# Selective scans on one core: two x buffers, one evacuation per projection, y summed in column quarters, and zero products counted at two passes

## The chip, the cores and the metric

One core of a Trainium2 chip runs the whole program. The metric is device time in microseconds of one execution: 15255.39 us as the median of three runs (15252.08 to 15267.42). The core has a TensorE (PE) for matrix products, a VectorE (DVE), a ScalarE (ACT), a GpSimd (POOL) and a SyncE (SP, which issues most DMAs). Each engine takes its instructions in the order in which the program stands for it, so one instruction that waits holds up all that stand behind it on that engine.

## The reference, cut to what matters

The model has four layers on `x` of shape 4 x 64 x 64 x 96. Layers 0 and 1 hold nearly all of the time: each runs four selective scans (in four orders of the 4096 tokens) over 192 channels with 16 states per channel, for 4 images. Layers 2 and 3 and the feed-forward parts come behind the scans and are untouched by the change. The core of a scan, cut from the reference:

```python
xs    = x_flat[:, :, idx[k]]                       # tokens in the order of direction k
dts, Bs, Cs = split(einsum('bkdl,kcd->bkcl', xs, x_proj_weight))
delta = softplus(einsum('bkrl,kdr->bkdl', dts, dt_projs_weight) + bias)
h     = h * exp(delta * A) + (delta * u) * B       # for each token, 192 x 16 states
y     = einsum('bkdn,bkn->bkd', h, C)              # sum over the 16 states
```

In layer 0 (the "ordered" one) the directions are two diagonal snakes and two radial orders, so tokens are gathered and scattered; in layer 1 they are rows and columns, forwards and backwards.

## The kernel before, in words

**Batches, directions, segments, groups.** `Stream.run` makes 8 batches (layer 0 for images 0 to 3, then layer 1 for images 0 to 3). A batch has 4 directions of 4 segments; a segment is 1024 tokens (`SEG`). A segment's 192 x 16 = 3072 state rows are 24 groups of 128 partitions (32 channels by 4 states): 6 channel blocks `cb` by 4 state blocks `sg`. So there are 8 x 16 x 24 = 3072 groups.

**One group** is worked on by all engines in turn. ACT makes the decay `da` (L1072). DVE multiplies the spread input `u` by B into `t` (L1076, `enter`) and runs the recurrence into `h` (L1083, `recur`). ACT keeps the last state (L1094). POOL multiplies `h` by C into `hc` (L1098, `leave`). PE sums `hc` over states into the PSUM tile `y` (L1107, `collect`): two products of 128 x 512, each to one column tile of 32 of the PE array. `y` holds two channel blocks (a pair); after the second, ACT copies it to `yc` (L1136), PE turns it (L1148), ACT copies the rows into `spare` (L1152) and, once a segment, the rows are stored (a plain DMA from SP, or, for the first two directions of layer 0, eight indirect scatters from POOL, L1162). `u` is one PSUM tile with one buffer: PE's `spread` (L1065, two products of 512 columns) for a channel block can start only when DVE has done the last `t` of the block before, and DVE's next `t` waits for it.

**Preparing the next segment** goes on beside this (`prepare`). PE transposes the fetched tokens (L897), ACT copies them into `xs` (L908, or L913 one copy per diagonal run), PE projects (L934: four times two products into the single PSUM tile `m`), ACT evacuates each projection with several reads of `m` (absolute value into `sp_z` L947, positive part into `dt` L949, B and C rows L951 or L953), ACT computes a softplus from these (L991 to L1006), PE adds its four terms (L1014), ACT copies the sum (L1017), SP stores it to DRAM, POOL forms `dtu = dt * x` (L1023). SP then loads `dt` spread over partitions (`dts`) and B and C (`bc`). In the kernel before there is one `xs`, so the first transpose for a segment waits for both `dtu` of the one before.

**Who sets the order.** `Flow.run` writes all orders down when the program is built: it plays a list of operations with a supposed duration (`occ`), a latency, a due time, and a flag `hard` for those of the 24 groups, and each time puts the operation that can start soonest. It is a plan made beforehand; the chip only follows the order. Where PE would be idle for a time `gap` in the plan, `keep_busy` puts products by zero in (L1125: 96 x 32 by 256 columns), which add nothing to `y` and are there to keep PE at work. In the kernel before, their number is `(gap - 0.15) * 0.7 / 0.215`, and there are none while no sum of `y` is open (from the last `collect` of a pair to the first of the next).

**Between batches** (`side_by_side`) another planner (`Plan`) merges the finished batch and makes the front part of a batch to come; its buffers are `z_rows`, `xc`, `y_rows`, `yt`, `dx` and `halo`.

Of the kernel before, what the change touches and what calls it, by code (L numbers as in the profile page):

```python
# [113 lines left out]
class Op:  # L114


    def __init__(self, engine, occ, emit, deps=(), lat=0.15, due=None, hard=False, bank=0, after=0.0):
        self.engine, self.occ, self.emit, self.lat = engine, occ, emit, lat
        self.deps = [d for d in deps if d is not None]
        self.due, self.hard, self.bank, self.after = due, hard, bank, after  # L120
        self.users, self.left, self.seen = [], 0, 0.0


class Flow:
# [11 lines left out]
    def run(self):  # L136
# [22 lines left out]
        while left:  # L159
            best = None  # L160
            for engine, ops in ready.items():
# [7 lines left out]
                if strict and first:  # L169
                    limit = first[-1].due + drift - (3.2 if engine == "PE" else 0.5)  # L170
# [20 lines left out]
            if engine == "PE":  # L191
                self.fill(start - free[engine])
# [4 lines left out]
            free[engine] = start + op.occ  # L197
            done = start + op.occ
# [4 lines left out]
            for user in op.users:  # L203
                user.seen = max(user.seen, done if user.engine == engine else done + op.lat)
                user.left -= 1
                if not user.left:
                    ready[user.engine].append(user)
# [97 lines left out]
class Layer:  # L305


    def __init__(self, s, a, pre, x_in):
# [24 lines left out]
        self.bias_bc = None  # L333
        if self.ordered:
            self.bias_bc = k.t(w, [128, ND], pre + "dir_bc")
            nc.sync.dma_start(self.bias_bc[C:], a[pre + "dirBC"])
        conv_w = k.load(s.seg, a[pre + "conv_w"], "conv_w")
# [39 lines left out]
class Stream:  # L377
# [4 lines left out]
    def __init__(self, k, ctx, a, x, x1, y1):  # L382
# [20 lines left out]
        self.bc = k.t(w, [128, 2, NSG, SEG], "bc")  # L403
        self.zeros = k.t(w, [C, GC], "zeros")
        nc.gpsimd.memset(self.zeros, 0.0)

# [5 lines left out]
    def front(self, bt, plan, rings, first=None):  # L412
# [22 lines left out]
        def edges(s, st):  # L435

            halo = yield from take(self.tmp, [C, 2, HW], "halo", 2)
# [29 lines left out]
        def project(s, st):  # L467
# [31 lines left out]
            def outer(j):  # L499
# [6 lines left out]
                z = yield from take(self.tmp, [C, 2, CH], "z_rows", 2)  # L506
# [19 lines left out]
        def convolve(s, st):  # L526
            yield lambda: st.pad is not None
            xc = []
            for _ in range(C // GC):
                xc.append((yield from take(self.tmp, [128, CH], "xc", 3)))  # L530
# [26 lines left out]
            rows = yield from take(self.tmp, [128, 2, 4, DI], "y_rows", 1)  # L557
# [27 lines left out]
    def merge(self, bt, plan, rings):  # L585
# [29 lines left out]
        def times_d(n):  # L615

            x = yield from take(tmp, [128, T, DI], "dx", 1)
# [73 lines left out]
        def finish(n, acc, mv):  # L691
# [20 lines left out]
            yt = yield from take(tmp, [C, 2, CH], "yt", 1)  # L712
# [35 lines left out]
    def side_by_side(self, ahead, behind=None, flush=None, seg=None):  # L748
# [3 lines left out]
        plan, rings = Plan(), Rings(k)  # L752
        self.ended, self.idle = False, None
# [117 lines left out]
    def prepare(self, seg, base=0.0, before=None):  # L871
# [7 lines left out]
        def op(name, engine, occ, emit, deps=(), at=0.0, **kw):  # L879
            x = Op(engine, occ, emit, deps, due=base + at, **kw)  # L880
# [22 lines left out]
        def keep_x(j, parts):  # L903
            if (j, parts[0]) == (0, 0):
                seg.xs = k.t(self.seg, [C, 2, SEG], "xs")
# [9 lines left out]
        for j in range(0, SEG // 128, 2):  # L915
            here = [f for n, f in enumerate(seg.fetched) if len(seg.fetched) < 4 or seg.turned or n // 2 == j // 2]
            here.append(o.get(("X", j - 2)))
            if j == 0:
                here += [b.get(("u", h)) for h in range(2)]
# [18 lines left out]
        def split(half, j, what):  # L938
            if (half, j, what) == (0, 0, 0):
# [6 lines left out]
            if what == 0:  # L946
                nc.scalar.activation(v.z[:, half, cols], ps[:C], AF.Abs, bias=bias)  # L947
            elif what == 1:
                nc.scalar.activation(v.dt[:, half, cols], ps[:C], AF.Relu, bias=bias)  # L949
            elif lay.bias_bc is None:  # L950
                nc.scalar.copy(v.bc[:, cols], ps[C:])  # L951
            else:
                nc.scalar.activation(v.bc[:, cols], ps[C:], AF.Identity, bias=lay.bias_bc[C:, kd : kd + 1])  # L953

        last, chain = o["xs", SEG // 128 - 2], None
        for half in range(2):
            for j in range(2):
                at = 20.0 + 3.5 * (2 * half + j)
                free = []
                if (half, j) == (0, 0):  # L960
                    free = [b.get(n) for n in (("u", 0), ("u", 1), ("out", 0), ("out", 1), "bc_out", ("sum", 1, 1))]
# [13 lines left out]
                p = op(("z", half, j), "ACT", 0.6, partial(split, half, j, 0), [p], at=at + 2.0)  # L975
                if half == 0:
                    p = op(("z", half, j), "ACT", 0.63, partial(split, half, j, 2), [p], at=at + 3.0)
                op(("z", half, j), "ACT", 0.65, partial(split, half, j, 1), [p], at=at + 4.0, bank=-1)
# [7 lines left out]
        def low(half, what):  # L986
            if (half, what) == (0, 0):
                seg.dtu = k.t(self.seg, [C, 2, SEG], "dtu", bufs=2)
            z, r = v.z, seg.dtu
            if what == 0:  # L990
                nc.scalar.activation(z[:, half], z[:, half], AF.Exp, scale=-1.0)  # L991
            elif what == 1:
# [5 lines left out]
        for half in range(2):  # L998
            p = op(("low", half, 0), "ACT", 1.08, partial(low, half, 0), [o["z", half, 1], p], at=32.0 + 5.0 * half)
            p = op(("low", half, 1), "ACT", 1.08, partial(low, half, 1), [p], at=33.5 + 5.0 * half)  # L1000
            p = op(("low", half, 2), "ACT", 1.08, partial(low, half, 2), [p], at=35.0 + 5.0 * half)
# [6 lines left out]
        op("log", "ACT", 4.6, log, [o["low", 0, 2], o["low", 1, 2], b.get(("sum", 1, 1))], at=42.0)  # L1008
# [91 lines left out]
    def collect(self, gr):  # L1100

        nc, seg, cb = self.nc, gr.seg, gr.cb
        if gr.sg == 0 and cb % 2 == 0:
            seg.y = self.k.t(self.ps_y, [128, CH], "y")
        for part in range(2):
            at = (part * 2 + cb % 2) * GC
            nc.tensor.matmul(  # L1107
                seg.y[at : at + GC, :],
                self.gather_y,
                gr.hc[:, part * CH : (part + 1) * CH],  # L1110
# [4 lines left out]
        self.open = gr if gr.sg < NSG - 1 else None  # L1115

    def keep_busy(self, gap):


        gr = self.open  # L1120
        if gr is None:
            return
        at = gr.cb % 2 * GC
        for _ in range(int((gap - 0.15) * 0.7 / 0.215)):
            self.nc.tensor.matmul(  # L1125
                gr.seg.y[at : at + GC, :256],
                self.zeros,
                gr.seg.bt.lay.diag.rearrange("p h t c -> p (h t c)")[:, :256],
                start=False,
                stop=False,  # L1130
                tile_position=(0, at),
# [6 lines left out]
    def turn(self, seg, pair):  # L1138

        k, nc = self.k, self.nc  # L1140
        if pair == 0:
            seg.rows = self.spare()[:, : SEG // 128 * DI].rearrange("p (f t d) -> p f t d", f=2, d=DI)
        ps = seg.ps = k.t(self.ps, [128, CH // 128, 128], "m")
        fours = seg.bt.lay.ordered or seg.kd % 2 == 0
        for j in range(CH // 128):

            v = seg.ycs[pair][:, j::4] if fours else seg.ycs[pair][:, j * 128 : (j + 1) * 128]
            nc.tensor.transpose(ps[:, j, :], v, k.ident)  # L1148

    def keep_rows(self, seg, pair):  # L1150
        ps = seg.ps.rearrange("p j (f d) -> p f j d", f=2)
        self.nc.scalar.copy(seg.rows[:, :, :, pair * 64 : (pair + 1) * 64], ps)  # L1152

    def store(self, seg):

        nc, ops = self.nc, []
        rows = lambda: seg.rows.rearrange("p f t d -> p (f t) d")
# [11 lines left out]
        def whole():  # L1169
            at = self.start(seg)  # L1170
            dst = to[at : at + SEG, :].rearrange("(f p t) d -> p f (t d)", f=2, t=4)
            nc.sync.dma_start(dst, seg.rows.rearrange("p f t d -> p f (t d)"))
# [4 lines left out]
        if seg.bt.lay.ordered and seg.kd < 2:  # L1177
            return [Op("POOL", 1.25, partial(scatter, j), lat=4.0) for j in range(SEG // 128)]
# [5 lines left out]
    def batch(self, segs):  # L1184
# [15 lines left out]
        for n, seg in enumerate(segs):  # L1200
            base, o, nxt = n * length, seg.o, seg.next
            prev = segs[n - 1] if n else None
            if nxt:
# [3 lines left out]
                nxt.o["low", 0, 0].deps += [prev.o["spread", NCB - 1]] if prev else []  # L1207
# [7 lines left out]
            for i in range(NG):  # L1215
# [44 lines left out]
                for g2 in (groups[n, i - 1], gr):  # L1260
# [24 lines left out]
                    )  # L1285
                    tail = seg is last and g2.g >= NG - 2
                    if tail:
# [4 lines left out]
                        0.87,  # L1292
# [24 lines left out]
    def finish_pair(self, flow, seg, gr, prev, base):  # L1317
# [4 lines left out]
        def copy():  # L1322
            self.copy_y(seg)
            seg.ycs[pair] = seg.yc

        self.copied = flow.add("ACT", 0.5, copy, [gr.collect, self.turned[-2]], lat=0.2, due=at + 10.0)
        t = flow.add("PE", 0.5, partial(self.turn, seg, pair), [self.copied, *self.rows_free(seg, pair)], lat=0.25, due=at + 15.0, bank=1)
# [1060 lines left out]
```

## Time and profile before

The profiled execution took 15402.95 us, its span is 15401.2 us, and the runs' median is 15255.39 us: the profiled one is 148 us (1.0%) over the median. Mean granted PE clock: 0.937.

| what | from the views of the profile |
|---|---|
| busy: PE, DVE, ACT, POOL | 13827.4, 12827.4, 8327.7, 9203.3 us |
| before the first batch's scan | 0 to 386.2 us |
| batches of layer 0, first `t` to last `h` | 1350.0, 1331.0, 1337.2, 1325.4 us |
| batches of layer 1, first `t` to last `h` | 1302.1, 1293.6, 1301.2, 1294.5 us |
| stretches between batches | 211.8, 212.8, 225.3, 209.1, 159.7, 155.9, 98.7 us |
| behind the last scan | 3206.7 us |
| layer 0, direction 0, four batches | 357.6, 339.2, 344.5, 339.3 us |
| layer 0, direction 1 | 336.8, 338.4, 340.0, 337.0 us |
| layer 0, direction 2 | 331.5, 329.4, 328.7, 327.1 us |
| layer 0, direction 3 | 324.1, 324.0, 324.0, 322.1 us |
| layer 1, direction 0 | 325.5, 327.6, 328.6, 328.4 us |
| layer 1, direction 1 | 328.2, 321.9, 328.6, 322.0 us |
| layer 1, direction 2 | 324.3, 322.0, 322.0, 321.9 us |
| layer 1, direction 3 | 324.2, 322.2, 322.1, 322.1 us |

How to read it: a batch is 16 segments, a direction is 4 of them. The lengths are differences between the starts of L1076 instructions (and the end of the last L1083) on the profile's time axis. A busy share is the time in which an engine had at least one instruction running. Products of 32-bit numbers appear in the profile as two records each, so a product of the program is two PE rows. An arrow `<-` in a row names what ended the idle time before it.

### The profile page before, as it was taken

The page shows a single profiled execution, that of the slowest core. Times are in us where ns is not written, and L with a number is a line of the kernel's source. Part 1 is how long each engine was busy: PE and PEld are TensorE (multiplying, and loading weights), DVE is VectorE, ACT ScalarE, POOL GpSimd, SP SyncE. Part 2 cuts the span into 40 slices and gives each one's busy share as a digit, 9 for nine tenths or more (in the row PEclk, how much of TensorE's full clock was granted, in tenths as well). Part 3 has the DMA queues.
Part 4 walks back from the last instruction along what each step waited for, and adds up shares of the span by engine and source line. Part 5 has one row for each costly group of instructions (what it writes and reads, how often), then busy time and mean ns, then how long its engine had stood idle before and what let it go on. Part 6 is the DMA issues. An engine that isn't in the chain of part 4 may idle for free. (4 is left out here: it accounts for less than half of the span.)

```text
span 15401.2 us, 196660 instructions
## 1 busy us (share of the span) xinstructions
PE 13827.4 (90%) x74369; PEld 5096.1 (33%) x74369; DVE 12827.4 (83%) x9642; ACT 8327.7 (54%) x13421; POOL 9203.3 (60%) x4657
## 2 busy tenths in 40 slices
PE   8899899989998999899989998999899789998877
PEld 3233333333333333333333333333233244443344
DVE  1999799978997899799979997999899856555655
ACT  3666466646664666466656665666566423232333
POOL 0788678867886688667747774777577620000123
PEclk9999899989998999899989999999999999998888
DMA  2333433343334333433343334333433400000122
GB/s 67 117 113 125 150 111 111 126 148 112 111 127 146 106 118 128 148 116 117 123 152 124 118 124 152 126 118 120 156 119 120 142 10 11 19 15 12 52 72 71
DMA packets 662768, 1637.49 MB, mean 106 GB/s; under 512 B 102822, under 2 KB 268460, under 8 KB 658045
## 3 DMA queue, kind: packets, MB, share of 16 engines
q1 hardware_dynamic: 624956, 1549.37, 31.4%
q0 software_dynamic: 36864, 75.55, 1.7%
q8 instruction: 588, 9.63, 0.3%
q14 instruction: 360, 2.94, 0.1%
HBM read 1295.03 MB, written 329.58 MB: 105 GB/s over the span
## 5 line engine op out<-in xcount | busy, mean ns | idle before, releaser
L1098 POOL TENSOR_TENSOR hc<-h,bc 128x1024 f32<-128x1024 f32 x3072 | 7198.4, 2365 | 2216.1 <-DVE h L1083 1909.0
L1083 DVE TENSOR_TENSOR_SCAN h<-da,state,t 128x1024 f32<-128x1024 f32 x2304 | 5300.4, 2355 | 26.0 <-ACT state L1094 16.3
L1072 ACT ACTIVATE da<-dts,L_A_logs 128x1024 f32<-128x1024 f32 x3072 | 3520.0, 1151 | 1832.2 <-DVE h L1083 1786.7
L1076 DVE TENSOR_TENSOR t<-u,bc 128x1024 f32<-128x1024 f32 x3072 | 3629.8, 1239 | 267.6 <-PE u L1065 193.5
L1107 PE MATMUL y<-hc,gather_y 128*32 128x512 f32 x12288 | 3529.1, 620 | 311.9 <-POOL hc L1098 241.7
L1125 PE MATMUL y<-L_diag,zeros 96*32 96x256 f32 x7824 | 1986.3, 386 | 0.0
L1083 DVE TENSOR_TENSOR_SCAN h<-da,t 128x1024 f32<-128x1024 f32 x768 | 1717.4, 2287 | 17.3 <-ACT da L1072 9.1
L1065 PE MATMUL u<-dtu,spread 32*128 32x512 f32 x3072 | 1573.1, 632 | 120.0 <-DVE t L1076 109.2
L1125 PEld LDWEIGHTS y<-L_diag,zeros 96*32 96x32 f32 x7824 | 852.8, 111 | 1425.0 <-issue 926.1
L1107 PEld LDWEIGHTS y<-hc,gather_y 128*32 128x32 f32 x12288 | 595.8, 109 | 2021.1 <-issue 1029.1
L934 PE MATMUL m<-xs,proj 96*128 96x512 f32 (+1 forms) x2048 | 1070.2, 641 | 67.3 <-ACT spare L1152 32.5
L1642 DVE SCALAR_TENSOR_TENSOR hcv<-padv,taps,hcv 128x2048 f32<-128x2048 f32 x384 | 902.2, 2350 | 13.4
L1566 POOL MEMSET padp<- 128x2448 f32 x32 | 68.6, 2143 | 1400.8 <-PE d L1606 1378.3
L1023 POOL TENSOR_TENSOR dtu<-dt,xs 96x1024 f32<-96x1024 f32 x256 | 603.0, 2356 | 506.1 <-ACT dt L1017 501.1
L1606 PE MATMUL d<-padp,diag 32*32 32x512 f32 x25600 | 885.7, 601 | 2.0 <-ACT hcp L1621 2.0
L1065 PEld LDWEIGHTS u<-dtu,spread 32*128 32x128 f32 x3072 | 521.4, 188 | 943.6 <-issue 588.0
L1017 ACT COPY dt<-m 96x512 f32<-96x512 f32 x512 | 297.2, 580 | 694.5 <-PE m L1014 690.0
L1014 PE MATMUL m<-dtu,ident 96*96 96x512 f32 x1024 | 563.8, 632 | 72.7 <-ACT dt L1017 65.9
L1606 PEld LDWEIGHTS d<-padp,diag 32*32 32x32 f32 x25600 | 484.4, 103 | 369.8 <-issue 196.9
L934 PEld LDWEIGHTS m<-xs,proj 96*128 96x128 f32 (+1 forms) x2048 | 324.6, 181 | 770.6 <-issue 483.8
L947 ACT ACTIVATE sp_z<-m,L_dtb 96x512 f32<-96x512 f32 x512 | 350.0, 684 | 409.5 <-PE m L934 393.5
L1014 PE MATMUL m<-sp_log,ident 96*96 96x512 f32 x1024 | 539.2, 608 | 0.0
(275 smaller groups left out, 15495.8 us busy)
## 6 DMA issues: line engine op xcount, KB each, us to landing
bc<-bc_dram SPq DMA_DIRECT2D x1024, 512.0 KB
dts<-dt_dram SPq DMA_DIRECT2D x768, 512.0 KB
dt_dram<-dt SPq DMA_DIRECT2D x256, 384.0 KB
y_tok<-spare SPq DMA_DIRECT2D x64, 768.0 KB
dt<-y_tok SPq DMA_DIRECT2D x128, 384.0 KB
x_tok<-y_rows SPq DMA_DIRECT2D x32, 768.0 KB
z_t<-z_rows SPq DMA_DIRECT2D x64, 384.0 KB
dx<-x_tok SPq DMA_DIRECT2D x64, 384.0 KB
```

The costliest lines, as they stand in the source:

```text
L934: nc.tensor.matmul(v.ps, seg.proj[:, src, to], seg.xs[:, src, chunks[j]], start=src == 0, stop=src == 1)
L1014: nc.tensor.matmul(v.ps, k.ident[:C, :C], term[:, half, chunks[j]], start=at == 0, stop=at == 3)
L1023: nc.gpsimd.tensor_mul(seg.dtu[:, half], v.dt[:, half], seg.xs[:, half])
L1065: self.nc.tensor.matmul(seg.u[:, cols], self.spread[rows, :], seg.dtu[rows, half, cols], start=True, stop=True)
L1072: self.nc.scalar.activation(gr.da, gr.seg.dts[gr.cb], AF.Exp, scale=scale)
L1076: self.nc.vector.tensor_mul(gr.t, gr.seg.u, self.bc[:, 0, gr.sg, :])
L1083: self.nc.vector.tensor_tensor_scan(gr.h[:, order], gr.da[:, order], gr.t[:, order], start, op0=ALU.mult, op1=ALU.add)
L1098: self.nc.gpsimd.tensor_mul(gr.hc, gr.h, self.bc[:, 1, gr.sg, :])
L1107: nc.tensor.matmul(seg.y[at : at + GC, :], self.gather_y, gr.hc[:, part * CH : (part + 1) * CH], start=gr.sg == 0, stop=gr.sg == NSG - 1, ...
L1125: self.nc.tensor.matmul(gr.seg.y[at : at + GC, :256], self.zeros, gr.seg.bt.lay.diag.rearrange("p h t c -> p (h t c)")[:, :256], start=Fal ...
L1606: nc.tensor.matmul(pc[i][j * 32 : (j + 1) * 32, :], diag[mine, ON_PE.index(t), tap, :], pad[mine, j * 8 + dy : j * 8 + dy + 8, dx : dx + H ...
L1642: nc.vector.scalar_tensor_tensor(to, win, wt, to, op0=ALU.mult, op1=ALU.add)
```

## The change

- **Column quarters.** `collect` issues four products of 256 columns, one to each column tile, in place of two of 512. `y`'s layout, `turn`, `keep_rows` (two copies in place of one), `store` (pieces of half the length) and the scatter's index table follow from it.
- **Zero products.** Their number is `(gap - 0.1) * share / 0.43`, with `share` 0.75 before a `hard` operation and 0.9 otherwise, and they go on where no sum is open: into the half of `y` that is done, or into the next pair's tile `next_y` (taken early, once ACT's copy of the old one is done).
- **One evacuation per projection.** ACT reads each projection from `m` once (with a bias column for 128 partitions); the absolute value and the positive part are made from `dt` in SBUF, as two more operations of 1024 columns for each half.
- **Two x buffers.** Odd segments keep `xs` in the last two fifths of a new fixed tile `area`, whose space the buffers of `side_by_side` share; the first transpose waits for `dtu` of the segment before the last.
- **The planner's numbers.** All of `prepare` is due 8 us later; `collect` counts 0.46 us in place of 0.87; `leave` and the copy of `y` get a slack of 1.2 and 1.0 us; each scatter depends on the one before having landed (3.0 us); PE's margin before hard work is 3.4 in place of 3.2.

```diff
             if engine == "PE":
-                self.fill(start - free[engine])
+                self.fill(free[engine], start - free[engine], 0.75 if op.hard else 0.9)
...
             for user in op.users:
-                user.seen = max(user.seen, done if user.engine == engine else done + op.lat)
+                near = user.engine == engine and not op.lands
+                user.seen = max(user.seen, done if near else done + op.lat + op.slack)
...
+        self.area = k.t(w, [128, 7 * SEG], "area")
...
+        cut("z_rows", 2, C, h=2, t=CH)
+        cut("xc", 3, 128, t=CH)
+        cut("y_rows", 1, 128, f=2, t=4, d=DI)
+        cut("yt", 1, C, h=2, t=CH)
+        cut("dx", 1, 128, t=CH // 128, d=DI)
+        cut("halo", 2, C, e=2, w=HW)
...
-            x = Op(engine, occ, emit, deps, due=base + at, **kw)
+            x = Op(engine, occ, emit, deps, due=base + at + 8.0, **kw)
...
-                seg.xs = k.t(self.seg, [C, 2, SEG], "xs")
+                if seg.i % 2:
+                    seg.xs = self.area[:C, 5 * SEG :].rearrange("p (h t) -> p h t", h=2)
+                else:
+                    seg.xs = k.t(self.seg, [C, 2, SEG], "xs")
...
-                here += [b.get(("u", h)) for h in range(2)]
+                here += [before.before.o.get(("u", h)) for h in range(2)] if before and before.before else []
...
-            if what == 0:
-                nc.scalar.activation(v.z[:, half, cols], ps[:C], AF.Abs, bias=bias)
-            elif what == 1:
-                nc.scalar.activation(v.dt[:, half, cols], ps[:C], AF.Relu, bias=bias)
...
+            if half == 0:
+                nc.scalar.activation(v.both[:, 0, cols], ps, AF.Identity, bias=lay.bias_bc[:, kd : kd + 1])
             else:
-                nc.scalar.activation(v.bc[:, cols], ps[C:], AF.Identity, bias=lay.bias_bc[C:, kd : kd + 1])
+                nc.scalar.activation(v.dt[:, 1, cols], ps, AF.Identity, bias=bias)
...
-        for part in range(2):
-            at = (part * 2 + cb % 2) * GC
+        for part in range(4):
+            at = part * GC
             nc.tensor.matmul(
-                seg.y[at : at + GC, :],
+                seg.y[at : at + GC, cb % 2 * 256 : (cb % 2 + 1) * 256],
                 self.gather_y,
-                gr.hc[:, part * CH : (part + 1) * CH],
+                gr.hc[:, part * 256 : (part + 1) * 256],
...
-        for _ in range(int((gap - 0.15) * 0.7 / 0.215)):
+        for _ in range(int((gap - 0.1) * share / 0.43)):
...
+        elif self.vacant and now > self.vacant.fin + 0.5:
+            if self.next_y is None:
+                self.next_y = self.k.t(self.ps_y, [128, CH], "y")
+            y, start = self.next_y[:GC, :256], True
...
-            return [Op("POOL", 1.25, partial(scatter, j), lat=4.0) for j in range(SEG // 128)]
+            ops = []
+            for j in range(SEG // 128):
+                ops.append(Op("POOL", 1.25, partial(scatter, j), ops[-1:], lat=3.0))
+                ops[-1].lands = True
+            return ops
...
+                    g2.leave.slack = 1.2
...
-                        0.87,
+                        0.46,
                         partial(self.collect, g2),
```

The two programs' instruction lists give the counts: zero products in the scans 3912 before and 5472 after; `collect` 6144 products of 512 columns before and 12288 of 256 after; of POOL's 256 scatters, 72 follow another with no `leave` between before, and none after. The order of DVE's instructions in the scans is the same in both.

## The prediction

> **What bounds the kernel now.** I read the busy times by stretch first, since a mean over the span hides the stages. Columns: stretch, its length, then each engine's busy us (count), granted PE clock, DMA share.
>
> ```profile
> 386.20:743.80 357.60, 317.86 (x1031) 105.30 (x1032) 323.58 (x193) 222.16 (x468) 264.53 (x127) 0.92 0.35 115
> 743.80:1080.60 336.80, 315.69 (x1035) 103.56 (x1036) 322.89 (x193) 215.03 (x381) 289.36 (x153) 0.95 0.37 118
> 8378.20:8700.10 321.90, 303.11 (x1033) 99.34 (x1032) 321.90 (x193) 210.44 (x304) 243.24 (x105) 0.99 0.39 123
> ```
>
> The third row is a direction of layer 1: DVE is busy 321.90 of 321.90 us, so no order of the others can shorten it (80.5 us a segment). The first two, of layer 0, have the same DVE work in 357.6 and 336.8 us: DVE idles 34 and 14 us at a lower clock. Summing the table's directions against 321.9: layer 0 is over by 93.0, 64.6, 29.1 and 6.6 us (directions 0 to 3, four batches each), layer 1 by 22.5, 13.1, 2.6 and 3.0. That is the ceiling, 234.5 us. Next, who DVE waits for (us in total, times, longest), first in layer 0, then in layer 1:
>
> ```profile
> DVE t L1076 <- PE u L1065: 147.5, 91, 6.0
> DVE h L1083 <- ACT state L1094: 19.5, 12, 2.1
> ```
> ```profile
> DVE t L1076 <- PE u L1065: 46.0, 32, 7.0
> ```
>
> So DVE waits for PE's spread, 1.6 us at a time; the waits for ACT's state copies are few, and the change does not touch them. Why is PE late? The timeline around the longest wait, POOL first:
>
> ```profile
> 498.27 1.20 POOL L1162 DMA_INDIRECT y_tok<-spare,scan_idx  x1 [0.18 <-issue]
> 503.61 0.96 POOL L1162 DMA_INDIRECT y_tok<-spare,scan_idx  x1 [4.14 <-DMA y_tok<-spare,scan_idx]
> 504.59 4.66 POOL L1098 TENSOR_TENSOR hc<-h,bc 128x1024 f32<-128x1024 f32 x2
> ...
> 514.26 0.96 POOL L1162 DMA_INDIRECT y_tok<-spare,scan_idx  x1 [3.84 <-DMA y_tok<-spare,scan_idx]
> ```
> ```profile
> 517.67 1.92 PE L1107 MATMUL y<-hc,gather_y 128*32 128x512 f32 x4 [2.78 <-POOL hc L1098]
> ...
> 523.80 0.74 PE L1148 MATMUL m<-ident,yc 128*128 128x128 f32 x4 [0.69 <-ACT yc L1136]
> ...
> 528.23 1.05 PE L1107 MATMUL y<-hc,gather_y 128*32 128x512 f32 x4
> 529.11 1.25 PE L1125 MATMUL y<-L_diag,zeros 96*32 96x256 f32 x5
> ```
> ```profile
> 528.33 2.36 DVE L1076 TENSOR_TENSOR t<-u,bc 128x1024 f32<-128x1024 f32 x2 [5.99 <-PE u L1065]
> ```
>
> Cause one: a scatter right behind another holds POOL some 4 us until the first has landed (498.27 to 503.61 is 5.3 us); the `hc` behind it is late, PE's `collect` and everything behind that too, and DVE stands 5.99 us. Cause two is the clock. At 930 us PE waits for DVE with no sum open, so without zero products, and then runs at half clock:
>
> ```profile
> 933.96 3.42 PE L1065 MATMUL u<-dtu,spread 32*128 32x512 f32 x4 [2.88 <-DVE t L1076]
> ```
> ```profile
> 934.00:938.00 4.00, 4.00 (x5) 1.31 (x6) 4.00 (x2) 3.94 (x6) 3.53 (x3) 0.55 0.04 7
> ```
>
> Four records took 3.42 us; at full clock (504.44 us) the same four took 1.98. Cause three: a zero product is planned at 0.215 us, but five records above take 1.25 us at 0.386 mean each, so one starts every (1.25 - 0.386) / 4 = 0.22 us, and a product is two: 0.43. Each filled gap is overrun by about 0.7 x 2 - 1 = 40%.
>
> **The change part by part.** PE work a segment, in start-to-start times at full clock. A `collect` takes 529.11 - 528.23 = 0.88, of which the two products run together. Whether four run together shows in the front part's convolutions, 12 records side by side in different tiles:
>
> ```profile
> 7929.38 0.64 PE L542 MATMUL t<-spare,L_diag 32*32 32x512 f32 x8
> 7929.44 0.61 PE L542 MATMUL m<-spare,L_diag 32*32 32x512 f32 x4
> 7929.81 0.61 PE L542 MATMUL t<-spare,L_diag 32*32 32x512 f32 x5
> ```
>
> The next round starts after 0.43 us, with four column tiles in each row tile. So four quarters of 256 columns should take about 0.88 / 2 plus their weight loads, 0.46 (an estimate); the bounds are 0.44 and 0.88. That is 24 x 0.42 = 10.1 us less. Zero products go from 3912 / 128 = 30.6 to 42.8 a segment: 12.2 x 0.43 = 5.2 us more. PE is freed of 4.9 us in 80.5, and its plan is now right, which matters more: the overrun goes, worth up to 40% of 30.6 x 0.22 = 2.7 us of lateness a segment, in places where DVE may be next.
>
> TensorEngine Tiling, Instruction Overhead, in the Trainium skill speaks against quarters: about 60 cycles of overhead a matmul. Four more records a `collect` at the 2.4 GHz of its clock page would be 0.1 us, 2.4 us a segment, halving the relief; the convolutions' 12 records within 0.43 us don't show such a cost.
>
> *Scatters.* In the new order at least two `hc` (4.66 us, then the scatter's own 1.0) stand between two, against a landing of 5.3: the wait goes. In the old order 72 pairs stood together; the 123.5 us that POOL waited there are the most it can give back directly. In direction 1, two `hc`, a scatter and a gather come to 4.66 + 2 x 1.0 = 6.7 us, exactly two groups of DVE (6.74 at 502.05 to 508.79): POOL has no room to catch up, so I take half there.
>
> *Zeros where no sum is open.* They fill 2.88 us waits like the one above. The new waits: a zero product into `next_y` waits for ACT's copy of `yc`; behind it stand the next `collect` and the spread. The plan adds 1.5 us of safety; if the copy is later still, PE idles as it does today. I take 0, bounds 0 to 384 copies x 0.3 us that reach DVE in a tenth: 12 us lost. Of each gap 10 to 25% stays empty, some 1 us in a gap of 4.
>
> The Trainium skill's TensorE: Matmul & The Clock Gate, in HAM oscillation, calls for no PE-idle gap above about 3.4 us, by which the 2.88 us wait should not have halved the clock; the trace differs and decides. By the page the remnant is free; by the row it is a third of what hurts.
>
> *Evacuations.* ACT drops six or more reads of 0.68 us and gains four of 1.05: nothing in sum, hidden by ACT's 111 us idle in 321.9. `m` is free sooner, so PE's projections wait less (23.7 us in layer 0). `keep_rows` adds one copy, under 0.58 us x 384, in the same cover.
>
> *The preparation moved.* Its sums, ACT copies, SP's stores and loads (`bc_out`, `out`, `dts`) and POOL's two `dtu` go later: `dtu` moves in layer 0 from behind 14 and 17 of 24 `hc` to 17 and 20, some 10 us; in layer 1 the second x buffer lets it drift forward to behind 4 and 8. Before, `dts` was asked for at 55 of 80.8 us and the first `da` ran at 72: of 17 us, 7 are left. Zero, with up to 5 us a batch (40) lost if loads slow. The slacks of `leave` and of the copy, and PE's wider margin, only make the plan put a waiting product later; their price is in the same 0. Half-size store pieces (64 stores) hide under a DMA share of 0.36. Between batches DVE's order is the same; the shared `area` can hold the second segment's first x copies for a store of `yt`: 0, at most 3 us a batch, 24.
>
> *Sum.* Layer 0: three quarters of 93.0 = 70, half of 64.6 = 32, 0.7 of 29.1 = 20, half of 6.6 = 3; layer 1: 0.6 of 41.2 = 25 (two early PE waits a batch, and half-clock spells). Total 150 us. Profiled: 15403 - 150 = 15253. The median is 148 us lower, and nothing shows those lying in scan waits, so 15255 - 150 = **15105 us**. Bounds: all 234.5 gives 15021; losses of 76 on a quarter of the gain (38) give 15293.
>
> **The rivals.** (1) *Half the gain*: POOL stays full in directions 0 and 1 and the clock still falls. For: POOL is busy 289.36 of 336.8 us. Against: kd 3 without scatters is already near 321.9. 15255 - 70 = 15185. (2) *Slower: the clock gate takes over.* With fewer zeros a gap, PE drops to half clock once a segment in layer 1 too; a spread then takes 3.4 us for 2.0, late by 1.4, plus queue, say 2 us. 128 x 2 = 256 against 150: 15360. It decides from 150 / 128 = 1.2 us a segment. Against: the fill without an open sum covers the very waits that trip it now. (3) *The quarters don't run together*: two by two, 0.88 a `collect`, while the plan says 0.46: PE is 24 x 0.42 = 10 us a segment behind its plan, and the scatters' gain is eaten: 15255.
>
> **How the numbers follow.** Forecast 0.68; rival 1 0.17; rival 2 0.08; rival 3 0.07, of which 0.05 within and 0.02 above the bound of no change. The predicted time is the forecast's. Range 15035 to 15225: below lies almost the whole ceiling, above rivals 2 and 3. About 0.2% (30 us) can be told from no change: faster 0.85, same 0.05, slower 0.10.
>
> **What would show it.** Right: scatter waits for scatter near 0; layer 0's directions 0 and 1 near 328 and 329 us; PE waiting for DVE before a spread under 1 us; clock 0.98 or more in layer 0; a `collect`'s records all starting within 0.3 us. Wrong: directions of layer 1 over 322, new DVE waits for `da` or `bc`, or clock spells in layer 1.

## The result, and the profile after

The changed kernel is slower: 15448.5 us median (15439.3 to 15472.0, 4 runs) against 15259.0 (15252.1 to 15267.4) for the kernel before beside it; ratio 1.0126, 95% interval 1.0109 to 1.0144. The forecast was 15105 us. The profiled execution has a span of 15439.4 us and a mean granted clock of 0.892 (before: 0.937).

Batches of layer 0 take 1347.0, 1337.6, 1341.0, 1329.5 us: 11 us more in sum. Batches of layer 1 take 1349.3, 1340.4, 1347.5, 1349.1: 195 us more, 3.0 a segment. The stretches between batches are 156 us shorter in layer 0 than in the profile before. That is not the change: the kernel before took 15244 to 15259 us in four sets of runs and 15395 to 15405 in two (the sets of experiments ran on five different chips), and layer 0's stretches are at 198 to 226 us in every profile of these two, as in the profile before, and at 173 to 183 in every one of the others, so that each kernel below is given as a ratio to the kernel before in its own set.

Busy times by stretch, two directions of layer 0 and one of layer 1 (columns as in the prediction: the stretch, its length, busy us and count of PE, of PE's weight loads, of DVE, ACT and POOL, then the granted clock, the DMA share and GB/s):

```profile
378.20:723.70 345.50, 307.15 (x1470) 117.06 (x1470) 323.28 (x192) 219.53 (x464) 263.25 (x126) 0.87 0.36 119
723.70:1061.60 337.90, 310.28 (x1501) 116.88 (x1502) 322.99 (x193) 213.95 (x391) 290.95 (x153) 0.89 0.36 117
8277.20:8614.80 337.60, 316.79 (x1518) 118.74 (x1522) 322.97 (x192) 214.20 (x314) 243.75 (x105) 0.89 0.37 120
```

Layer 1's direction had DVE busy in all of its 321.9 us; now DVE idles 14.6 of 337.6, and the clock fell from 0.99 to 0.89. Whom DVE waits for, first in layer 0, then in layer 1:

```profile
DVE t L1109 <- PE u L1098: 180.3, 85, 6.4
...
DVE t L1109 <- PE u L1098: 236.1, 137, 7.0
```

It is the same wait, PE's spread; in layer 1 it was 46.0 us in 32 waits. One of them, in order of time, PE first, then ACT, then DVE:

```profile
8417.25 1.96 PE L963 MATMUL m<-area,proj 96*96 96x512 f32 x4
...
8422.23 0.66 PE L1189 MATMUL m<-ident,yc 128*128 128x128 f32 x4 [2.44 <-ACT dt L978]
8422.81 1.05 PE L1166 MATMUL y<-L_diag,zeros 96*32 96x256 f32 x4
8424.06 3.78 PE L1098 MATMUL u<-dtu,spread 32*128 32x512 f32 x4 [0.20 <-DVE t L1109]
8427.76 1.94 PE L1141 MATMUL y<-hc,gather_y 128*32 128x256 f32 x16
8429.63 3.73 PE L963 MATMUL m<-area,proj 96*96 96x512 f32 x4
...
8438.88 3.19 PE L1166 MATMUL y<-L_diag,zeros 96*32 96x256 f32 x14
8441.99 1.98 PE L1098 MATMUL u<-dtu,spread 32*128 32x512 f32 x4
...
8416.90 1.06 ACT L1013 ACTIVATE sp_z<-dt 96x1024 f32<-96x1024 f32 x1
8417.98 1.06 ACT L1015 ACTIVATE sp_z<-sp_z 96x1024 f32<-96x1024 f32 x1
8418.95 1.04 ACT L1017 ACTIVATE dt<-dt 96x1024 f32<-96x1024 f32 x1
8419.89 0.56 ACT L1177 COPY yc<-y 128x512 f32<-128x512 f32 x1
8420.36 1.15 ACT L1105 ACTIVATE da<-dts,L_A_logs 128x1024 f32<-128x1024 f32 x1
8421.41 0.18 ACT L1127 COPY state<-h 128x1 f32<-128x1 f32 x1
8421.49 0.68 ACT L978 ACTIVATE dt<-m,L_dtb 96x512 f32<-96x512 f32 x1
...
8435.14 2.34 DVE L1109 TENSOR_TENSOR t<-u,bc 128x1024 f32<-128x1024 f32 x2
8437.39 4.58 DVE L1116 TENSOR_TENSOR_SCAN h<-da,state,t 128x1024 f32<-128x1024 f32 x2
8444.01 2.36 DVE L1109 TENSOR_TENSOR t<-u,bc 128x1024 f32<-128x1024 f32 x2 [2.04 <-PE u L1098]
```
```profile
8420.00:8423.90 3.90, 1.64 (x8) 0.78 (x8) 3.90 (x3) 3.83 (x8) 3.72 (x2) 1.00 0.15 50
8423.90:8437.00 13.10, 12.94 (x39) 4.34 (x40) 13.10 (x9) 7.80 (x10) 7.75 (x4) 0.50 0.35 119
```

Read it in three steps. ACT takes its list in order: absolute value, exponential, positive part, a `yc` copy and a decay run before the evacuation at 8421.49. The projection had ended at about 8419.2, so the only bank `m` stays taken for 2.3 us more and PE's turn stands 2.44 us. (The two operations that the change added, L1013 and L1017, are 2.1 us of what stands ahead.) Then the clock goes from 1.00 to 0.50 for 13.1 us (second fence): the spread takes 3.78 us for 1.98, the projections 3.73 for 1.96. PE falls behind its list; and at 8438.88 it works off 14 records of zeros, 3.1 us, which the plan had put into a gap that PE, being late, no longer has. DVE had released `u` with its last `t` at 8437.5; the spread begins at 8441.99, and DVE stands 2.04 us.

The scatters did what was foretold. GpSimd in layer 0's direction 1:

```profile
780.41 1.01 POOL L1205 DMA_INDIRECT y_tok<-spare,scan_idx  x1
782.22 2.34 POOL L1131 TENSOR_TENSOR hc<-h,bc 128x1024 f32<-128x1024 f32 x1 [0.80 <-DVE h L1116]
...
790.67 1.00 POOL L1205 DMA_INDIRECT y_tok<-spare,scan_idx  x1 [0.15 <-issue]
```

The waits of some 4 us for a landing are gone. And quarters run four together:

```profile
8443.90 1.07 PE L1141 MATMUL y<-hc,gather_y 128*32 128x256 f32 x16
8444.79 1.46 PE L1166 MATMUL y<-L_diag,zeros 96*32 96x256 f32 x6
```

The 16 records of `collect`, two groups, are followed by the next work after 0.89 us, 0.45 each.

### The profile page after: what moved, and what is told of

Same layout as the page of the kernel before. It is cut to its first block, busy times and chain, and to the rows that moved or that the text cites. A ratio compares the mean times of both kernels' runs of the same rounds, so it can differ in the third digit from the quotient of the medians.

```text
span 15439.4 us, 227490 instructions
## 1 busy us (share of the span) xinstructions
PE 13798.6 (89%) x89777; PEld 5606.5 (36%) x89777; DVE 12858.7 (83%) x9645; ACT 8293.1 (54%) x13549; POOL 9210.9 (60%) x4657
## 5 line engine op out<-in xcount | busy, mean ns | idle before, releaser
L1109 DVE TENSOR_TENSOR t<-u,bc 128x1024 f32<-128x1024 f32 x3072 | 3596.4, 1216 | 491.7 <-PE u L1098 416.4
L1166 PE MATMUL y<-L_diag,zeros 96*32 96x256 f32 x10944 | 2898.7, 400 | 3.7 <-ACT yc L1177 3.7
L1141 PE MATMUL y<-hc,gather_y 128*32 128x256 f32 x24576 | 2366.8, 431 | 61.4 <-POOL hc L1131 60.2
L1098 PE MATMUL u<-dtu,spread 32*128 32x512 f32 x3072 | 1784.4, 706 | 300.4 <-DVE t L1109 293.7
L1166 PEld LDWEIGHTS y<-L_diag,zeros 96*32 96x32 f32 x10944 | 1153.6, 114 | 1627.4 <-issue 751.4
L1141 PEld LDWEIGHTS y<-hc,gather_y 128*32 128x32 f32 x24576 | 743.1, 116 | 1731.8 <-issue 1244.6
L1056 POOL TENSOR_TENSOR dtu<-dt,xs 96x1024 f32<-96x1024 f32 x128 | 302.1, 2360 | 504.3 <-ACT dt L1050 504.1
L963 PE MATMUL m<-xs,proj 96*128 96x512 f32 (+1 forms) x1024 | 575.5, 681 | 21.2 <-ACT xs L937 11.0
L963 PE MATMUL m<-area,proj 96*128 96x512 f32 (+1 forms) x1024 | 574.7, 679 | 20.3 <-ACT dt L976 12.0
L1047 PE MATMUL m<-dt,ident 96*96 96x512 f32 x1024 | 571.3, 641 | 0.0
L1047 PE MATMUL m<-sp_z,ident 96*96 96x512 f32 x1024 | 570.9, 641 | 0.0
```

Source lines behind the costliest of these rows:

```text
L963: nc.tensor.matmul(v.ps, seg.proj[:, src, to], seg.xs[:, src, chunks[j]], start=src == 0, stop=src == 1)
L1047: nc.tensor.matmul(v.ps, k.ident[:C, :C], term[:, half, chunks[j]], start=at == 0, stop=at == 3)
L1098: self.nc.tensor.matmul(seg.u[:, cols], self.spread[rows, :], seg.dtu[rows, half, cols], start=True, stop=True)
L1109: self.nc.vector.tensor_mul(gr.t, gr.seg.u, self.bc[:, 0, gr.sg, :])
L1141: nc.tensor.matmul(seg.y[at : at + GC, cb % 2 * 256 : (cb % 2 + 1) * 256], self.gather_y, gr.hc[:, part * 256 : (part + 1) * 256], start=g ...
L1166: self.nc.tensor.matmul(y, self.zeros, lay.diag.rearrange("p h t c -> p (h t c)")[:, :256], start=start, stop=start, tile_position=(0, 0),)
```

## The experiments

All runs in one table. "zeros 3.3/us" means 3.3 zero products for each us of planned gap; the changed kernel has 1.7 to 2.1, the kernel before 3.3. The columns "layer 0" and "layer 1" are the mean length of a batch's scans in each layer, from each profile (in us; before: 1335.9 and 1297.9, clock 0.937; DVE waits for spreads 193.5 us in all; changed: 1338.8, 1346.6, 0.892, 416.4). Times in the expectations were written against 15259 us; the ratios are to be compared.

| run | kernel | ratio, 95% interval | layer 0 | layer 1 | clock | DVE waits for `u` |
|---|---|---|---|---|---|---|
| e5 | changed, again | 1.0125, 1.0108-1.0142 | 1344 | 1342 | 0.890 | 420.1 |
| e1 | changed, zeros 3.3/us | 1.0653, 1.0635-1.067 | 1398 | 1492 | 0.932 | 1191.9 |
| e2 | changed, zeros 2.6/us | 1.0338, 1.032-1.0355 | 1358 | 1419 | 0.924 | 755.3 |
| e6 | changed, half the zeros | 1.0194, 1.0157-1.0231 | 1352 | 1365 | 0.828 | 546.0 |
| e10 | changed, zeros in open sums only | 1.0132, 1.0108-1.0156 | 1349 | 1322 | 0.848 | 367.1 |
| e11 | changed, halves | 1.0126, 1.0109-1.0142 | 1348 | 1333 | 0.916 | 396.8 |
| e7 | changed, old evacuations | 1.0091, 1.0074-1.0108 | 1339 | 1325 | 0.893 | 333.6 |
| e8 | changed, one x, due as before | 1.0084, 1.0067-1.0101 | 1334 | 1334 | 0.896 | 347.6 |
| e16 | changed, old evacuations and due, two x | 1.0127, 1.0103-1.0151 | 1335 | 1340 | 0.893 | 377.3 |
| e9 | changed, old preparation (e7 + e8) | 0.9987, 0.9975-0.9999 | 1321 | 1319 | 0.895 | 222.1 |
| e13 | e9 with halves | 0.9989, 0.9979-0.9998 | 1332 | 1303 | 0.925 | 171.3 |
| e14 | e9 without slacks | 0.9974, 0.9964-0.9984 | 1314 | 1308 | 0.921 | 185.5 |
| e15 | e9, zeros in open sums only | 1.007, 1.0053-1.0087 | 1339 | 1331 | 0.854 | 315.1 |
| e12 | e9, as e14 and e15 together | 1.0224, 1.0198-1.025 | 1361 | 1354 | 0.862 | 527.0 |
| e3 | before, zeros 1.9/us | 1.0007, 0.9996-1.0018 | 1341 | 1302 | 0.915 | 214.7 |
| e4 | before, scatters' chain | 0.9929, 0.9913-0.9946 | 1309 | 1303 | 0.942 | 130.8 |
| e17 | e13 without slacks | 0.9908, 0.9889-0.9927 | 1309 | 1292 | 0.940 | 85.9 |
| e18 | e17, old count in open sums | 0.9965, 0.9947-0.9982 | 1312 | 1315 | 0.953 | 178.3 |

**The number of zeros.** e1, e2 and e6 change one expression in `keep_busy`:

```
-        for _ in range(int((gap - 0.1) * share / 0.43)):
+        for _ in range(int((gap - 0.15) * 0.7 / 0.215)):          # e1
+        for _ in range(int(gap * 1.1 / 0.43)):                    # e2
+        for _ in range(int((gap - 0.1) * share * 0.5 / 0.43)):    # e6
```

> The changed kernel with the old number of zero products a gap (3.3 for each us of gap, against 1.7 to 2.1); where they go and all else stays changed. Theory F (too few zeros: TensorE idles inside the gaps and falls to half clock): the mean granted clock returns from 0.89 to 0.93 or more, batches of layer 1 fall from 1349, 1340, 1348, 1349 us towards 1300, the time to 15120-15250 us. Theory E (the single evacuation and the two further ScalarE reads hold the one bank m, TensorE stands before a turn and halves there, whatever the gaps hold): clock 0.89-0.90, layer 1 over 1335 a batch, time 15400-15480 us.

> The changed kernel with gaps filled to 110% by the changed price of 0.43 us a product (2.6 for each us of gap, between the changed and the old number). Theory F: most of what the old number gives back, 15130-15280 us; if the overrun of the old number costs as the prediction said, 20-60 us faster than with the old number. Theory E: no change, 15400-15480 us.

> The changed kernel with half of its zero products (0.9 to 1.0 for each us of gap), in the same places. Theory Z (TensorE's queue is in order and full of zero products: a spread that DVE has just released stands behind them; more zeros were slower in the two fuller kernels): DVE's wait for spreads falls from 416 to under 300 us and the time by 70-200 us against the changed kernel. Theory F (too few zeros, half clock): the clock falls below 0.87 and the time is 100 us or more above the changed kernel's.

Theory F fell with e1: the clock did return, to 0.932, and the kernel became 6.5% slower than the kernel before, where the changed one is 1.3% slower; e2 lies between. Theory E, which had both unchanged, missed as well. The profile of e1 has the reason, in the row of `t` (busy and mean ns, then idle time and what ended most of it):

```profile
L1109 DVE TENSOR_TENSOR t<-u,bc 128x1024 f32<-128x1024 f32 x3072 | 3609.4, 1221 | 1267.2 <-PE u L1098 1191.9
```

DVE's wait for spreads grew from 416.4 to 1191.9 us. Z, in its turn, fell with e6: half the zeros are also slower, at a clock of 0.828, and the wait for spreads, which Z had at under 300 us, grew to 546.0. More zeros and fewer both cost, and the changed number lies between them.

**The same number in the kernel before** (e3), `int((gap - 0.1) * 0.8 / 0.43)` for the old count:

> The kernel before with its zero products thinned to the changed number (1.9 for each us of gap); the order of all else is untouched. Theory F: the granted clock falls from 0.94 to 0.89-0.90, layer 1 from about 1298 to 1330-1350 us a batch, time 15400-15500 us. Theory E: the old evacuations keep the bank moving, so the time stays within 60 us of 15259.

No difference. In this kernel a smaller overrun and a lower clock (0.915 for 0.937) come to nothing together; whether each is worth nothing or the two cancel was not tried apart.

**The scatters alone** (e4): of the change, only this, with the lines in `Flow.run` that make `lands` count:

```
+            for j in range(SEG // 128):
+                ops.append(Op("POOL", 1.25, partial(scatter, j), ops[-1:], lat=3.0))
+                ops[-1].lands = True
```

> The kernel before with the scatters' chain alone (each planned behind the landing of the one before). By the prediction's ceiling for it, up to 100 us of layer 0 come back: 15155-15230 us, the batches of layer 0 at 1310-1325. Rival: GpSimd's waits for the scatters were hidden or come back as later hc, and the time stays within 30 us of 15259.

15297.9 us against 15405.4: 108 us, with layer 0's scans 27 us a batch shorter (directions 0, 1 and 2 by 59, 34 and 18 us over four batches, direction 3 longer by 4).

**The preparation.** e5 is the changed kernel once more. e7 puts the three reads of `m` and the three further operations back, and with them which of these waits for the previous segment's last sum and spread; e8 the one `xs`, its wait for `("u", h)` of the segment before, and `due=base + at`; e9 both; e16 is e9 with the two x buffers kept. The main lines of e7, and the due time of e8:

```
-            if half == 0:
-                nc.scalar.activation(v.both[:, 0, cols], ps, AF.Identity, bias=...)
-            else:
-                nc.scalar.activation(v.dt[:, 1, cols], ps, AF.Identity, bias=bias)
+            if what == 0:
+                nc.scalar.activation(v.z[:, half, cols], ps[:C], AF.Abs, bias=bias)
+            elif what == 1:
+                nc.scalar.activation(v.dt[:, half, cols], ps[:C], AF.Relu, bias=bias)
...
-            x = Op(engine, occ, emit, deps, due=base + at + 8.0, **kw)
+            x = Op(engine, occ, emit, deps, due=base + at, **kw)
```

> The changed kernel once more, beside the others of this set. The kernel before took 15259 us in the runs beside the changed one and 15405 in those beside the first four experiments, so the base has to be taken again. If the surplus is in the scans: ratio to before 1.010-1.015 again, batches of layer 1 at 1340-1350 us. If the changed kernel only shares the longer stretches between batches of that set: the same ratio at a longer time.

> The changed kernel with the three evacuations of the kernel before (Abs, B and C, Relu read from the bank m) in place of the single one and its two further SBUF operations. Theory E (the single evacuation queues behind Abs, Exp and Relu, so the bank m is held and TensorE stands some 2.4 us before a turn and halves): the wait of the turn for the evacuation (111 us in 51 waits) all but goes, layer 1 falls from 1347 to 1300-1320 us a batch, the time by 100-180 us. Theory Z: at most 60 us, since the zeros ahead of the spreads stay.

> The changed kernel with one x buffer (the next segment's x waits for the previous one's dtu, as before) and the preparation due 8 us sooner, as before. Theory P (the second buffer lets the preparation drift forward until ScalarE stands on the dtu buffer, 173 us of waits for TensorE's spread, with evacuations behind it): layer 1 falls by 20 us a batch or more, the time by 80-200 us. Theory Z or E: within 60 us of the changed kernel.

> The changed kernel with both preparation edits undone (three evacuations, one x buffer, due 8 us sooner); quarters, zero products, scatters and slacks stay changed. Each undone alone gave 62 and 67 us. If they are separate terms: 15300-15330 us, layer 1 at 1305-1320 a batch. If both act through one overloaded stretch of ScalarE and TensorE, one undoing has had most of it: 15350-15385 us. If the preparation is the whole loss, the scatters' gain shows and the time is below the kernel before's.

> The changed kernel with the old evacuations and the old due time, two x buffers kept. If the second buffer's early drift is what spoils: as e7, 1.006-1.010. If it was the later due time: near e9, 0.996-1.003.

e5 repeats the loss, 1.0125, with layer 1 at 1342 us a batch: it lies in the scans. The two edits undone singly give 62 and 67 us, together some 210. Put onto e9, the single evacuation costs 0.97% (e8 less e9, 148 us of 15255), the second x buffer 1.40% (e16 less e9, 214 us), and either leaves little for the other, which suggests that they spoil the same thing. With the old evacuations the due time is no part of the loss: with it at 8 us later e7 is 0.36% faster than e16. DVE's waits for spreads, in e9 and in e16:

```profile
DVE t L1100 <- PE u L1089: 222.1, 150, 10.1
DVE t L1103 <- PE u L1092: 377.3, 187, 10.6
```

The turn's waits for the evacuation, in the changed kernel and in e7:

```profile
PE m L1189 <- ACT dt L978: 110.8, 51, 2.5
PE m L1183 <- ACT dt L978: 9.9, 14, 1.4
```

All waits of the turn fall by less, from 291.9 to 163.6 us, since those for the copies into the x buffers, which hold `m` too, grow from 61.9 to 118.5. Layer 1 falls by 22 us a batch to 1325: less than E had, and the time by 62 us, at the bound of what Z allowed (60). E is a part of the loss, not the whole.

**Quarters.** e11 puts `collect`, `turn`, `keep_rows`, `store` and the index table back to halves, planned at 0.87; e13 does so in e9:

```
-        for part in range(4):
-            at = part * GC
+        for part in range(2):
+            at = (part * 2 + cb % 2) * GC
```

> The changed kernel with sums of y in halves at 0.87 us planned (the old collect, turn, copy of the rows and stores); everything else stays changed. Prediction's term: quarters free TensorE of 10 us a segment, so halves are slower, 15480-15600 us. Theory Q (the freed time goes into zero products anyway, and the plan with 0.46 draws other work forward): within 40 us of the changed kernel, or faster.

> The kernel of e9 (old preparation) with sums in halves at 0.87 planned. Prediction's term: quarters free TensorE of 10 us a segment, so halves lose: above 1.005. Theory Q (freed time is no gain: it is filled with zeros, or idles and halves the clock): halves as good or better, 0.985-0.998, below e4's 0.9929 if the slacks and the zeros without an open sum are gains.

Equal to the kernels with quarters, both times. A `collect` does take half as long, and it is worth nothing here; without slacks halves are ahead (e17 below, 0.9908, against e14, 0.9974, in two sets).

**Zeros without an open sum, and slacks.** e10 and e15 return from `keep_busy` when no sum is open; e14 leaves out `slack = 1.2`, `slack = 1.0` and the margin of 3.4; e12 both:

> The changed kernel with zero products only while a sum is open, as before, at the changed number a gap. Theory F (the clock falls in unfilled waits): the clock below 0.89 and 15460 us or more. Theory Z (zeros stand ahead of spreads): the ones without an open sum are a part of them, 15380-15430 us.

> The kernel before with the scatters' chain, the quarters at 0.46 and the changed number of zero products, these only where a sum is open; the preparation, the slacks and the margin are the old ones. The scatters alone gave 0.9929 of the kernel before. If quarters are a gain or nothing: ratio 0.980-0.993. If quarters and their thin fill are themselves a loss: above 0.996, layer 1 over 1310 us a batch.

> The kernel of e9 without the slacks (1.2 behind hc, 1.0 behind the copy of y) and with the old margin of 3.2. If the slacks hold the quarters up (without them TensorE stands for hc, 540 us in e12 against 55 in e9): most of the 345 us between e9 and e12, ratio 1.015-1.025. If it is the zeros without an open sum: 0.997-1.003.

> The kernel of e9 with zero products only while a sum is open; slacks stay. If the zeros without an open sum make the 345 us: 1.015-1.025. If the slacks do: 0.997-1.005, as in the changed kernel, where leaving these zeros out moved the time by less than 0.2%.

In e9 these zeros are a gain of 0.83% (127 us, e15 against e9); in the changed kernel, within the intervals, they are worth nothing (e10: by its profile, of a run 52 us under its median, layer 1 gains 25 us a batch and layer 0 loses 11). Without slacks e9 is level (0.9974 against 0.9987, the intervals overlap). Without both it is 2.4% slower: an interaction, neither guess was right. In e12 PE stands 540 us for `hc` (55.0 us in e9), and the clock is 0.862; but e14 has 314 us of the same wait at 0.921 and no loss, so it takes both. The row of e12:

```profile
PE y L1132 <- POOL hc L1122: 539.8, 437, 4.0
```

**A better version.** e17 is e13 without slacks; e18 has the old number of zeros in open sums:

> Scatters' chain, old preparation, halves, no slacks: the kernel of e4 with the changed number of zero products, also where no sum is open. If the new filling is a gain in halves too: below 0.9929. If the number is too low for halves: 0.995-1.000.

> The kernel of e17 with the old number of zero products in open sums; where no sum is open the changed number. Against e4 it adds only the zeros without an open sum. If they are a gain (127 us with quarters): 0.985-0.990 and the best of all. If the overrun then has no gap left to run into, as in the two fuller kernels: above 1.000.

e17 is 0.9% faster than the kernel before, and so faster than the changed one; its interval overlaps that of e4, so the new filling on top of the scatters is not shown as a gain. e18 shows that in halves too the old overrun costs (0.57%) once there are zeros without an open sum. e17 by stretch, a direction of layer 0 and one of layer 1, and its DVE row:

```profile
373.50:707.80 334.30, 298.69 (x999) 98.04 (x1000) 322.83 (x193) 221.72 (x468) 264.25 (x127) 0.95 0.37 122
8229.20:8551.20 322.00, 305.92 (x1014) 95.04 (x1012) 322.00 (x194) 211.41 (x304) 243.14 (x105) 0.98 0.38 122
```
```profile
L1100 DVE TENSOR_TENSOR t<-u,bc 128x1024 f32<-128x1024 f32 x3072 | 3598.7, 1219 | 160.0 <-PE u L1089 85.9 <-DMA bc<-bc_dram 73.2
```

DVE is again busy in all of a layer 1 direction, and its spread waits are below half of those before.

## Why the prediction was wrong

In ratios the loss of 1.26% has three parts: the scatters' chain gives 0.71% (e4); quarters, slacks and the new zeros cost 0.58% on top of it (e9 against e4); the two edits of the preparation cost 1.39% on top of that (the changed kernel against e9). The forecast was a gain of 0.98%, 150 us, with the preparation at zero.

- **Evacuations: the step that failed.** "Nothing in sum, hidden by ACT's 111 us idle in 321.9. `m` is free sooner" counted ACT's time and not its order. The two operations moved into SBUF stand ahead of the next evacuation in ACT's list, so `m` is free later. The whole edit costs 148 us (e8 against e9); a kernel with only these two operations moved in the list was not run.
- **The preparation moved: failed too.** "Zero, with up to 5 us a batch" priced loads. The second x buffer alone costs 214 us; the loads did not appear among DVE's waits. Its cause is only partly seen: in late spreads PE does more preparation first (table below), and in layer 1 of e16 PE's sums wait 42 us, 43 times, for the copy of `dt` that holds `m` (under 3 us in e9), and its projections 16 us for copies into the second x buffer (2 in e9). DVE's waits rise from 222.1 to 377.3 us. Which of the moved instructions does it was not tried.
- **PE work: right in size, wrong in worth.** Quarters take 0.45 us (0.46 estimated), so rival 3 did not come. But PE's time was not what bounded, and e11 and e13 put the gain at none. So the "4.9 us in 80.5" should not have carried any part of 150 us.
- **Scatters: right.** 108 us alone, with 59 and 34 in layer 0's directions 0 and 1, where 70 and 32 were forecast for the whole change. The changed kernel loses it again in layer 0: its batches are 11 us over those before.
- **Zero overrun 40%: wrong in worth.** e3 gains nothing. The 2.7 us a segment are also small by the prediction's own numbers: the gaps that 30.6 products fill come to 30.6 x 0.215 / 0.7 = 9.4 us, and 40% of that is 3.8.
- **Zeros where no sum is open, "I take 0":** a gain of 127 us in e9, nothing in the changed kernel. **Slacks, "in the same 0":** they cost 0.8% with halves (e13 against e17, two sets); with quarters no cost is shown (e14).
- **Rival 2** named the place and nearly the price: layer 1 lost 3.0 us a segment, 2 were written, 1.2 were needed. Half clock did come, but fewer zeros a gap was not the cause of the loss: more zeros are far slower (e1), and e9 has nearly as much half-clock time as the changed kernel.

What replaces it: PE's waits in layer 1's scans are as long in sum as before (those over 0.3 us: 335 us, was 322) but fewer and longer (239, was 321). In both layers' scans the clock is at half for 2113 us, was 519 (spells that lie wholly in a batch's scans); half of that is lost to PE, 8.3 us a segment against 2.0; the difference is 6 of the 10.1 that quarters free.

What PE did meanwhile can be added up from the traces. Taken are the spreads in layer 1's scans for which DVE stood over 0.3 us (a batch's first left out), and the time from DVE's release of `u` (the end of the last `t` that read it) to the spread's first record. Preparation is PE's transposes, projections and sums for the next segment.

| kernel | late spreads | release to spread, us | zeros | preparation | `collect` and turn | idle |
|---|---|---|---|---|---|---|
| before | 25 | 81 | 24 | 34 | 20 | 3 |
| changed | 119 | 424 | 216 | 118 | 60 | 29 |
| e9 | 71 | 250 | 126 | 101 | 19 | 3 |
| e8 (e9 and the single evacuation) | 91 | 336 | 142 | 147 | 32 | 15 |
| e16 (e9 and the second x buffer) | 98 | 376 | 132 | 193 | 37 | 14 |
| e1 (changed, 3.3 zeros/us) | 333 | 1491 | 1026 | 247 | 114 | 105 |
| e17 | 9 | 32 | 5 | 18 | 8 | 1 |

Of each such stretch the first 2.6 us are free at full clock, since DVE's next two `h` take 4.58 us and the spread 1.98; so the table says what stood ahead of the spread, and not what each costs. In the changed kernel half of it is zeros, in e16 half is preparation. Of the spreads' own 316 us in the changed kernel 169 ran at half clock.

My reading is that PE has no reserve there, so that waits and work which the preparation edits add end in late spreads. The runs show the parts' prices; that the missing reserve links them is read from the traces, not isolated by a run: e9 has 1938 us at half clock and yet stands level with the kernel before. One difference lies in what came before these spells (the longest PE wait that ended in the 3.5 us before each, in layer 1): in e9 it is 102 times of 152 a wait of the spread for DVE, when PE is ahead, and 41 times one of the turn for `m`; in the changed kernel 37 times of 126 the first and 65 times the second.

## What to carry to other kernels

Cost an edit on an in-order engine by who waits behind the moved instructions, above all where one PSUM bank passes through that engine; idle time in sum does not cover it. Freeing an engine that is not the bound was no gain by itself, and filler work in an in-order queue can stand ahead of late work: here its right amount changed from kernel to kernel (3.3 and 1.9 were level in the kernel before, and 5% apart in the changed one). Run the parts alone: here one was worth 108 us, and two others cost 148 and 214 us each on top of the rest.

## What the runs showed of the hardware

- In the scans of the kernel before, the changed one, e4, e9, e14, e16 and e17, of 336 PE waits of 2.1 us or more that began at full clock, 328 were followed by half clock within 3 us of their end; of 365 waits of 1.5 to 2.1 us, 270; of 974 of 0.9 to 1.5 us, 252; of 2611 of 0.3 to 0.9 us, 330. The Trainium skill's TensorE: Matmul & The Clock Gate, in HAM oscillation, puts the limit at gaps of about 3.4 us; in these traces waits well below it are followed by half clock.
- All 1158 half-clock spells that lie wholly in these scans last a whole multiple of 3.41 us, 427 of them one and 318 two; those of the changed kernel last 8.7 us on average (2113 us in 242). So a wait of some 2 us that is followed by half clock loses PE an estimated 1.7 us of work or more (half of 3.41), if it has any to do. A spread of four records takes 1.98 us at full clock and 3.78 at half.
- Four products of 128 x 32 by 256 columns in four column tiles take 0.45 us together, two of 512 columns in two column tiles 0.88.
